# A Newton-iteration and spectral-convolution kernel: earlier loads and another cadence for the inverse transforms, and filler matmuls at the end

## The chip, the cores and the metric

The kernel runs on one core of a Trainium2 chip. The metric is the device time of one execution in microseconds (us), taken as the median of several runs; lower is better. All data is 32-bit floating point.

## What is computed

The input `x` holds 32 images of 32 channels of 128 x 128 numbers. Two layers follow each other, each a residual step on a group-normalised input:

```
def _L0_conv_ref(A):                       # a matrix square root for each 128x128 channel
    normA = jnp.sqrt(jnp.sum(A2 * A2, axis=(1, 2)))
    Y = A2 / normA[:, None, None]; Z = I
    for _ in range(5):
        T = 0.5 * (3.0 * I - jnp.matmul(Z, Y))
        Y = jnp.matmul(Y, T)
        Z = jnp.matmul(T, Z)
    return Y * jnp.sqrt(normA)[:, None, None]

def _L1_conv_ref(x, weights1, weights2):   # a spectral convolution, 32 modes each way
    x_dht = jnp.fft.fftn(x.astype(jnp.complex64), axes=(2, 3)).real
    top = jnp.einsum('bixy,ioxy->boxy', x_dht[:, :, :M1, :M2], weights1)
    bot = jnp.einsum('bixy,ioxy->boxy', x_dht[:, :, -M1:, :M2], weights2)
    # top and bot are put into an otherwise zero spectrum
    y = jnp.fft.ifftn(out_dht.astype(jnp.complex64), axes=(2, 3)).real
    return y

x = x + _L0_conv_ref(_gn(x))
x = x + _L1_conv_ref(_gn(x), L1_conv_weights1, L1_conv_weights2)
```

## The kernel before, in words

**Layer 0.** The unit of work is a *quad*: four channels of one image, so 256 quads in all. `newton` (L426) carries a quad through a chain of small matrix products on TensorE (PE), whose results VectorE (DVE) and ScalarE (ACT) bring back from PSUM; GpSimd (POOL) adds the identity (`r<-mb,eye`, `r<-b,eye`). It ends with the product `ps<-y,t` and the DVE add `xt<-ps,xt`. `settle` (L458) writes the finished quad to the DRAM scratch `mid` (issued by SP) and folds it on POOL (`fold<-xt`).

**Layer 1.** `forward`, `summed` and `spectrum` make an image's spectrum. The images are cut into groups of 20, 7, 3 and 2 (`GROUPS`, L43). When a group's spectra are complete, `wide_products` (20), `small_products` (7 and 3) or `last_products` (2) multiply them by the weights, mode by mode, and write the products to the DRAM scratch `od`. Then `inverse` (L887) takes the images of the group one by one: `load_products` (SP, `ob<-od` or `or<-od`), `place` (ACT, puts small groups' products in order, `ob<-or`), two banks of matmuls `ps<-tab,ob` copied by ACT to `gt`, and then for each half `e` of the channels eight matmuls `ps<-gt,tab`, ACT copies to `d`, DVE adds `yt<-ps,yt`, and `unfold` (POOL `yt<-yt,d`, 8 channels at a time, two instructions). `store` issues the finished 8 channels to `out`. `yt` are the image's own rows, read back from `mid` by `load_input(b, e)` (L832), two transfers of 512 KB for each half; they come from a pool of six buffers, in turn.

**What sets the order.** Nothing is scheduled at run time: every engine gets its instructions in the order in which the Python program issues them (`InOrder`, L68), and each engine, SP's queue too, holds at an instruction whose semaphores are not ready. The program is a loop of *rounds* (L1042 on). In each round every lane (up to nine, at most five quads under way in the last images) gives one step of its quad, and in between one step each of the queues `preps`, `specs`, `posts`, `prods` (the products) and `backs` (the inverses) is taken. The last images start a quad every 5 rounds (`NEAR`). A step of `inverse` ends at each `yield`. Before, these lines set the pace:

```
            if i == 0 and rounds % 3 or tail:
                step(prods)
            if i == 0 and (rounds % 3 == 0 or holding) or tail and not (posts or specs):
                step(backs)
```

so `backs` has every third round and, by `holding`, the round after the first quarter of each half; `prods` has the other two rounds. An image of a group takes six steps: one in which it only sees that its loads were issued, one for `ps<-tab,ob`, and two for each half. Counting through the loop this makes 12 rounds an image. The second half's rows are loaded at the end of the first half (`if not e: load_input(b, 1)`), two rounds ahead of the DVE adds that use them. `tail` is true once no quad is left or under way: then every queue is stepped for each lane. Stores are issued by SP, in the tail by ACT.

**Buffers that matter at the end.** `page` is a pool of three tiles shared by `om` (products on their way to `od`), `d` and `or`. PSUM is a ring of eight banks (`bank`). While the last quads run, `weights` (L782) also sends 28 weight tiles of 256 KB through SP's queue into Newton buffers that have come free.

Of the kernel before, what the change touches and what calls it, by code (L numbers as in the profile page):

```python
# [88 lines left out]
def conv_preact_kernel(  # L89
# [77 lines left out]

    def bank():
        return ps8.tile([P, 4, P], F32, tag="ps", name="ps")

    def root(v, n, tag):

# [154 lines left out]
    def products(lhsT, rhs):  # L327
        ps = bank()
        for j in range(4):
            nc.tensor.matmul(ps[:, j, :], lhsT[:, j], rhs[:, j], start=True, stop=True)  # L330
        return ps
# [94 lines left out]
    def newton(g, sn, xt, m, mb, far, more):  # L426


        q = yield from quartic(m, mb, far, more, False)
        my = four("my", more)  # L430
        y = my[:, :, 0, :]
        nc.scalar.mul(y, products(q, m), 1 / (MS * QF))
        yield from rest
        m = my[:, :, 1, :]
        nc.scalar.mul(m, products(q, y), MS / QF)
        yield from rest
        mb = taken(transposed(m), "mb", more)
        yield from rest
        q = yield from quartic(m, mb, far, more, True)
        both = [bank().rearrange("p (j k) x -> p j k x", k=2) for _ in range(2)]  # L440
        for j in range(4):
            nc.tensor.matmul(both[j // 2][:, j % 2], q[:, j], my[:, j], start=True, stop=True)
        w, y = four("t", more), four("y4", more)
        for h in range(2):
            nc.scalar.mul(w[:, 2 * h : 2 * h + 2, :], both[h][:, :, 1, :], 1 / (MS * QF))
        for j in range(4):
            c = 4 * g + j
            nc.scalar.mul(y[:, j, :], both[j // 2][:, j % 2, 0, :], sn[:, c : c + 1])
        yield from rest
        t = plus(products(w, q), -0.5 * EYE / (1.5 * QF), eye, "t", more)  # L450
        yield from rest
        nc.vector.tensor_tensor(xt, products(t, y), xt, ALU.add)
        yield

    folds = {}
# [88 lines left out]
    def spectrum(b, u):  # L544


        uv = u.rearrange("p q c a (t e l) -> p a e t (q c) l", e=2, l=4)
        ps = [bank() for _ in range(2)]
        for a in range(2):
            for i in range(2):  # L550
                for e in range(2):
                    rows = slice(64 * i, 64 * i + 64)
                    nc.tensor.matmul(
                        ps[i][64 * e : 64 * e + 64, 0:2, :],
                        tab[rows, T_FH.start + a * K : T_FH.start + (a + 1) * K],
                        uv[rows, a, e],
                        start=(a == 0),
                        stop=(a == 1),
                    )
        z = sp.tile([P, 4, P], F32, tag="sp", name="z", bufs=2)  # L560
        for i in range(2):
            nc.scalar.copy(
                z.rearrange("p t (l i c) -> p t l i c", i=2, c=G)[:, :, :, i, :],
                ps[i].rearrange("p a x -> p (a x)")[:, 0:256].rearrange(
                    "p (t c l) -> p t l c", c=G, l=4
                ),
            )
        yield
        v, r = scales.pop(b)
        ps = transposed(z)  # L570
        spec = sp.tile([P, 4, P], F32, tag="sp", name=f"spec{b}", bufs=2)
        spec = spec.rearrange("p a x -> p (a x)").rearrange("p (k q t) -> p k q t", q=4, t=8)
        nc.scalar.activation(
            spec.rearrange("p k q t -> p t (k q)"),
            ps.rearrange("p t (e k) -> p (t e) k", e=2),
            AF.Identity,
            scale=r,
        )
        yield
        nc.vector.scalar_tensor_tensor(  # L580
            spec[0:C, 0, 0, 0:1], v[0:C, 1:2], r[0:C], spec[0:C, 0, 0, 0:1], ALU.mult, ALU.add
        )
        yield
        i, j = where[b]
        if i == len(xs):

            for e, t in enumerate(diags):
                for l4 in range(4):
                    rows = slice(32 * l4, 32 * l4 + 32)
                    copy = nc.scalar.copy if l4 % 2 else nc.vector.tensor_copy  # L590
                    copy(
                        t.rearrange("p (m b l f) -> p m b l f", b=2, l=4, f=4)[rows, :, j, l4, :],
                        spec[rows, 8 * e : 8 * e + 8].rearrange("p k q (h f) -> p (k q h) f", f=4),
                    )
            yield
            return
        kept(
            nc.sync.dma_start(
                out=xs[i][:, :, j, :].rearrange("k p m -> p k m"),
                in_=spec.rearrange("p (k e) q t -> p k (e q t)", e=KK // xs[i].shape[0]),  # L600
            )
        )
        yield
# [136 lines left out]
    def last_products(i):  # L740


        for e in range(2):
            load_input(B - GROUPS[i], e)
        for kk in range(KK):
            if kk % 4 == 0:
                yield
                om = page(f"om{i}_{kk}").rearrange("p (f s o) -> p s f o", f=4, s=8)
            if kk % 2 == 0:
                pm = bank()  # L750
            for h in range(2):
                if kk < 2:
                    wt = plain[kk][:, 512 * h : 512 * h + 512].rearrange("p (q x) -> p q x", q=4)
                else:
                    wt = late_wts[2 * kk - 4 + h]
                for q in range(4):
                    m = 8 * (kk % 8) + 2 * q + h
                    nc.tensor.matmul(
                        pm[32 * q : 32 * q + 32, 2 * (kk % 2) + h, :],
                        diags[kk // 8][:, 32 * m : 32 * m + 32],  # L760
                        wt[:, q, :],
                        start=True,
                        stop=True,
                    )
            if kk % 2:
                half = kk % 4 // 2
                copy = nc.vector.tensor_copy if half else nc.scalar.copy
                copy(
                    om[:, 4 * half : 4 * half + 4], pm.rearrange("p s (f o) -> p s f o", f=4)
                )  # L770
            if kk % 4 == 3:
                for f in range(4):
                    queue = nc.scalar if f % 2 else nc.sync
                    kept(
                        queue.dma_start(
                            out=od[i][f, kk - 3 : kk + 1].rearrange("k r x -> r k x"),
                            in_=om[f::4, :, f, :].rearrange("p (k h) o -> p k (h o)", h=2),
                        )
                    )
        yield  # L780

    def weights():  # L782
# [49 lines left out]
    def load_input(b, e):  # L832

        if b >= B or (b, e) in yts:
            return
        yts[b, e] = []
        for i in range(2):
            o = 16 * e + 8 * i
            turn = len(yts) + i
            if len(settled) == B * C // 4 and not folds and turn % 3 == 2:  # L840
                y = sets.tile([P, 8, P], F32, tag="fold", name=f"yt{b}_{o}", bufs=3)
            else:
                y = inv.tile([P, 8, P], F32, tag="yt", name=f"yt{b}_{o}", bufs=6)
            kept(nc.sync.dma_start(out=y, in_=mid[b][:, o : o + 8, :]))
            yts[b, e].append(y)
# [3 lines left out]
    def store():  # L849
        while stores:  # L850
            b, o, y = stores.pop(0)
            kept((nc.scalar if tail else nc.sync).dma_start(out=out[b, :, o : o + 8, :], in_=y))
# [34 lines left out]
    def inverse(b):  # L887


        more = where[b][1] < GROUPS[where[b][0]] - 1  # L890
        load_products(b)
        load_input(b, 0)
        yield
        if b not in placed:
            place(b)
            if not tail:
                yield
# [12 lines left out]
        for e in range(2):  # L910
            gts.append(inv.tile([P, 4, P], F32, tag="gt", name=f"gt{b}_{e}", bufs=3))
            nc.scalar.copy(gts[e], pg[e])
        unfold()
        yield
        for e in range(2):
# [16 lines left out]
            for i in range(2):  # L932
# [11 lines left out]
                if not i:  # L944
                    holding.append(b)
                    yield
                    holding.pop()
            if not e:
                load_input(b, 1)
            elif more:  # L950
                load_input(b + 1, 0)
                place(b + 1)
            yield
        if not more:
            unfold()
# [86 lines left out]
    while todo or any(lanes) or posts or specs or prods or backs:  # L1042
# [3 lines left out]
        for i in range(LANES):  # L1046
# [26 lines left out]
                step(specs)  # L1073
            if i == 3 or tail:
                step(posts)
            if i == 0 and rounds % 3 or tail:
                step(prods)
            if i == 0 and (rounds % 3 == 0 or holding) or tail and not (posts or specs):
                step(backs)
        rounds += 1  # L1080

# [68 lines left out]
```

## Time and profile before

Every instruction is recorded through one helper, so all have line L83 (`keep_in_program_order`) and are told apart by the tiles that they write and read.

| | |
|---|---|
| median of 3 runs | 3040.89 us (3040.22 to 3058.99) |
| the profiled execution's own time | 3037.9 us |
| its span on the core | 3035.8 us |
| PE busy, weight loads apart | 2878.3 us, 95% of the span |
| DVE, POOL, ACT busy | 2263.7, 1987.6, 1644.0 us |
| POOL `yt<-yt,d` | 242 instructions, 304.3 us, 1280 ns each |
| DVE `yt<-ps,yt` | 256 instructions, 682 ns each (median) |
| mean granted TensorE clock | 0.983 |

In the timeline a row gives the start, the duration, the engine, the operation with its tiles and shapes, how many equal instructions it merges, and in brackets the engine's idle time before it and what ended that. SPq and ACTq rows are the issuing of transfers. The windows view gives, for each stretch, its length and then each engine's busy time and instruction count, the granted clock, the DMA engines' mean share and GB/s.

### The profile page before, as it was taken

How to read it: one execution, taken by the hardware profiler on the slowest of the kernel's cores; microseconds unless marked ns; L12 is line 12 of the kernel's file. 1: busy time of each engine (PE TensorE's matmuls, PEld its weight loads, DVE VectorE, ACT ScalarE, POOL GpSimd, SP SyncE). 2: the span in 40 equal slices, each digit the busy share in tenths (PEclk: the TensorE clock that was granted, in tenths of full speed). 3: DMA queues.
4: the chain of work that ended last, by engine and by line, in shares of the span. 5: the costliest groups of instructions: out<-in, count | busy, mean ns of one | idle time of the engine just before them, and what ended most of it. 6: DMA issues, size and time to landing. Idle time of an engine off the chain costs nothing. (4 is left out here: it accounts for less than half of the span.)

```text
span 3035.8 us, 73213 instructions
## 1 busy us (share of the span) xinstructions
PE 2878.3 (95%) x27076; PEld 2675.2 (88%) x27076; DVE 2263.7 (75%) x4261; ACT 1644.0 (54%) x4187; POOL 1987.6 (65%) x2306
## 2 busy tenths in 40 slices
PE   6999999999999999999999999999999999898973
PEld 6899999999999999999999889889888889797863
DVE  6778787878787888778876656877778767776654
ACT  3566565665656665565644445555555555564442
POOL 4577677777777776767765435678777774675542
PEclk9999999999999999999999999999999999999986
DMA  5576676777675768575733567667667677575585
GB/s 173 163 231 206 213 215 214 215 214 222 201 232 189 240 190 247 182 240 185 246 109 105 169 205 233 234 215 254 235 205 258 230 249 241 178 233 179 183 265 187
DMA packets 476658, 636.39 MB, mean 210 GB/s; under 512 B 97040, under 2 KB 257296, under 8 KB 476304
## 3 DMA queue, kind: packets, MB, share of 16 engines
q1 hardware_dynamic: 362400, 422.21, 43.3%
q10 hardware_dynamic: 113904, 209.50, 22.3%
q8 instruction: 217, 3.56, 0.5%
q14 instruction: 137, 1.12, 0.1%
HBM read 402.42 MB, written 229.11 MB: 208 GB/s over the span
## 5 line engine op out<-in xcount | busy, mean ns | idle before, releaser
L83 PE MATMUL ps<-my,q 128*128 128x128 f32 (+1 forms) x4096 | 736.4, 329 | 12.7 <-DVE v L83 9.8
L83 PEld LDWEIGHTS ps<-my,q 128*128 128x128 f32 x4096 | 625.8, 191 | 71.5 <-DVE v L83 11.4
L83 POOL TENSOR_TENSOR w<-w,r 128x512 f32<-128x512 f32 x288 | 366.7, 1275 | 379.2 <-DMA w<-turn 308.7
L83 PE MATMUL ps<-w,v 128*128 128x128 f32 x4096 | 552.5, 278 | 25.1 <-DVE w L83 12.4
L83 ACT ACTIVATE b<-b,a_off,a_sc 128x128 f32<-128x128 f32 x1024 | 469.8, 492 | 173.1 <-issue 47.5
L83 POOL TENSOR_TENSOR fold<-xt 128x256 f32<-128x256 f32 x512 | 363.3, 731 | 285.0 <-DVE xt L83 256.2
L83 PEld LDWEIGHTS ps<-w,v 128*128 128x128 f32 x4096 | 503.2, 193 | 40.0 <-DVE w L83 11.8
L83 ACT ACTIVATE my<-ps 128x512 f32<-128x512 f32 x512 | 306.1, 604 | 351.1 <-PE ps L83 333.7
L83 DVE SCALAR_TENSOR_TENSOR q<-ps,eye 128x512 f32<-128x512 f32 x512 | 350.4, 685 | 180.6 <-PE ps L83 175.8
L83 POOL TENSOR_TENSOR yt<-yt,d 128x512 f32<-128x512 f32 x242 | 304.3, 1280 | 273.1 <-ACT d L83 240.7
L83 ACT ACTIVATE t<-ps 128x256 f32<-128x256 f32 x512 | 191.2, 382 | 356.6 <-PE ps L83 345.7
L83 POOL TENSOR_TENSOR r<-mb,eye 128x512 f32<-128x512 f32 x256 | 326.3, 1275 | 79.1 <-ACT mb L83 79.1
L83 POOL TENSOR_SCALAR x<-xt,a_nm,a_sc 128x128 f32<-128x128 f32 x736 | 321.6, 450 | 21.3 <-DVE a_n L83 18.7
L83 POOL TENSOR_TENSOR r<-b,eye 128x512 f32<-128x512 f32 x256 | 326.5, 1275 | 2.7 <-ACT b L83 2.7
L83 ACT ACTIVATE y<-ps,a_t_s 128x128 f32<-128x128 f32 x1024 | 291.2, 375 | 0.0
L83 PE MATMUL ps<-x,b 128*128 128x128 f32 x2048 | 274.9, 278 | 7.5 <-POOL x L83 5.7
L83 PE MATMUL ps<-x,q 128*128 128x128 f32 x2048 | 274.4, 277 | 4.0 <-DVE q L83 2.2
L83 PE MATMUL ps<-y,t 128*128 128x128 f32 x2048 | 273.8, 277 | 2.3 <-DVE t L83 2.3
L83 PE MATMUL ps<-my,mb 128*128 128x128 f32 x2048 | 273.6, 277 | 0.4 <-DVE q L83 0.4
L83 PE MATMUL ps<-q,t 128*128 128x128 f32 x2048 | 274.1, 277 | 0.0
L83 DVE STREAM_TRANSPOSE turn<-v 128x512 f32<-128x512 f32 x288 | 264.9, 920 | 9.9
L83 PEld LDWEIGHTS ps<-x,b 128*128 128x128 f32 x2048 | 251.3, 193 | 11.0 <-POOL x L83 6.0
(121 smaller groups left out, 4481.1 us busy)
## 6 DMA issues: line engine op xcount, KB each, us to landing
turn<-turn SPq DMA_DIRECT2D x288, 256.0 KB
b<-in_x ACTq DMA_DIRECT2D x256, 256.0 KB
xt<-in_xt ACTq DMA_DIRECT2D x256, 256.0 KB
xs<-in_xs ACTq DMA_DIRECT2D x256, 256.0 KB
mid<-xt SPq DMA_DIRECT2D x256, 256.0 KB
yt<-mid SPq DMA_DIRECT2D x128, 512.0 KB
out<-yt SPq DMA_DIRECT2D x113, 512.0 KB
w<-turn SPq DMA_DIRECT2D x144, 256.0 KB
```

Source lines behind the costliest of these rows:

```text
L83: return self.tc.keep_in_program_order(issue(*args, **kw))
```

## The change

The inverses get fixed rounds of ten (0, 3 and 7) instead of every third. A step that only waited for loads is dropped for all images but the first of a group, so an image takes five steps, which is 10 rounds. The second half's rows are loaded in the step of the image's first matmuls, ahead of which the stores that are ready are issued; stores are also issued after a `holding` round. In the tail the two last images' products are loaded together and placed before the first one's output. `warm(n)` puts n matmuls of 128 x 512 whose results nobody reads into TensorE's queue: 2 after the last quad's last product, 2 ahead of the last group's products, 9 after them.

```
+    def warm(n):
+        ps = bank()
+        for _ in range(n):
+            nc.tensor.matmul(ps, ident, tab[:, 0:512], start=True, stop=True)
...
         nc.vector.tensor_tensor(xt, products(t, y), xt, ALU.add)
+        if not todo and lanes.count(None) == LANES - 1:
+            warm(2)
         yield
...
+            if tail:
+                warm(2)
             yield
             return
         kept(
...
+        warm(9)
         yield
 
     def weights():
...
         more = where[b][1] < GROUPS[where[b][0]] - 1
-        load_products(b)
-        load_input(b, 0)
-        yield
         if b not in placed:
+            load_products(b)
+            if tail and more:
+                load_products(b + 1)
+            load_input(b, 0)
+            yield
             place(b)
...
             nc.scalar.copy(gts[e], pg[e])
+        if tail and more:
+            place(b + 1)
+        store()
+        load_input(b, 1)
         unfold()
         yield
...
                     yield
                     holding.pop()
-            if not e:
-                load_input(b, 1)
-            elif more:
+                    store()
+            if e and more:
                 load_input(b + 1, 0)
-                place(b + 1)
+                if b + 1 not in placed:
+                    place(b + 1)
             yield
...
-            if i == 0 and rounds % 3 or tail:
+            turn = rounds % 10 in (0, 3, 7)
+            if i == 0 and not turn or tail:
                 step(prods)
-            if i == 0 and (rounds % 3 == 0 or holding) or tail and not (posts or specs):
+            if i == 0 and (turn or holding) or tail and not (posts or specs):
                 step(backs)
```

## The prediction

> **What bounds the kernel now.** I read the page first, then windows cut at each image's first inverse matmul, then the timeline at TensorE's three largest late gaps.
>
> ```profile
> span 3035.8 us, 73213 instructions
> PE 2878.3 (95%) x27076; PEld 2675.2 (88%) x27076; DVE 2263.7 (75%) x4261; ACT 1644.0 (54%) x4187; POOL 1987.6 (65%) x2306
> ...
> PE   6999999999999999999999999999999999898973
> PEclk9999999999999999999999999999999999999986
> ```
>
> TensorE is full until the last two slices, so in the body only its idle time can be won; after about 2939 us it is idle for long stretches and its clock falls. In the inverses' stretch I cut windows from one image's `ps<-tab,ob` to the next's:
>
> ```profile
> 1934.50:1962.20 27.70, 27.70 (x251) 25.27 (x250) 20.24 (x40) 15.38 (x42) 21.82 (x26) 1.00 0.68 233
> 2086.50:2116.10 29.60, 29.60 (x259) 26.83 (x258) 24.07 (x52) 16.01 (x43) 22.89 (x27) 1.00 0.77 265
> 2180.00:2217.10 37.10, 31.53 (x259) 28.51 (x258) 28.11 (x44) 17.36 (x48) 24.19 (x30) 0.91 0.58 188
> 2247.60:2277.80 30.20, 30.20 (x267) 27.60 (x266) 19.98 (x35) 16.30 (x43) 24.68 (x29) 1.00 0.75 248
> 2400.10:2430.80 30.70, 30.41 (x265) 27.37 (x264) 27.19 (x53) 16.37 (x44) 24.78 (x29) 1.00 0.66 222
> ```
>
> These are images 2, 7, 10, 12 and 17. Length less PE busy is idle time: 0 to 0.3 us in four, 5.6 us in image 10, where the next images' statistics fall on POOL's `yt<-yt,d`. Over images 0 to 25, less 19 (its window holds products), the idle time adds up to 34 us. The largest gap comes after image 26's first half:
>
> ```profile
> 2787.94 2.36 SPq L83 DMA_DIRECT2D out<-yt  x3
> ...
> 2791.59 2.17 SPq L83 DMA_DIRECT2D yt<-mid  x2
> ...
> 2799.80 1.29 DVE L83 TENSOR_TENSOR yt<-ps,yt 128x512 f32<-128x512 f32 x2 [11.55 <-DMA yt<-mid]
> ...
> 2801.74 3.69 PE L83 MATMUL ps<-my,q 128*128 128x256 f32 x8 [9.83 <-DVE v L83]
> ```
>
> The second half's load left SP late, behind the small group's `diag<-xs` issues and three stores; DVE waited at its head, a Newton step's `v` stood behind it, and TensorE starved. The same happens to image 28 at the last quad:
>
> ```profile
> 2938.51 2.35 SPq L83 DMA_DIRECT2D out<-yt  x3
> 2941.16 5.83 SPq L83 DMA_DIRECT2D yt<-mid  x2
> ...
> 2950.03 1.29 DVE L83 TENSOR_TENSOR yt<-ps,yt 128x512 f32<-128x512 f32 x2 [11.72 <-DMA yt<-mid]
> ...
> 2954.32 1.40 POOL L83 TENSOR_TENSOR fold<-xt 128x256 f32<-128x256 f32 x2
> 2955.77 1.97 PE L83 MATMUL ps<-fold,tab 128*32 128x504 f32 x12 [16.25 <-POOL fold L83]
> ```
>
> After that all is one chain to the end: spectrum, products, `od` and back, two inverses.
>
> ```profile
> 2980.85 9.06 SPq L83 DMA_DIRECT2D od<-om  x6
> 2987.91 0.59 ACT L83 COPY om<-ps 128x512 f32<-128x512 f32 x1 [9.86 <-DMA od<-om]
> ...
> 2997.30 3.07 SPq L83 DMA_DIRECT2D or<-od  x4
> ...
> 3003.01 1.05 ACT L83 COPY ob<-or 128x512 f32<-128x512 f32 x1 [6.58 <-DMA or<-od]
> ...
> 3016.85 2.08 PE L83 MATMUL ps<-tab,ob 64*128 64x128 f32 x16 [6.45 <-DVE ob L83]
> ```
>
> The third `om` waits for a page whose write to `od` stood in SP's queue behind image 30's loads; the last image's matmuls wait until `ob` is placed at the very end of the one before.
>
> **What the Trainium skill says.** "TensorE: Matmul & The Clock Gate", section "The HAM clock gate": an idle window of about 3.4 us halves TensorE's clock until it has been busy about as long. The trace agrees: after the 16 us gap the twelve fold matmuls take 1.97 us, where a like group took 1.09 at 2911.70. "SBUF — State Buffer", section "SBUF: two separate sides": VectorE with two SBUF inputs and GpSimd lock one port pair for a whole instruction. It agrees: DVE's 128 x 1 `b_inv` takes 4.34 us at 1917.29, beside POOL's `yt`, and 0.16 us at 2883.24. "DMA: Bandwidth & Descriptors", section "Issuing engines are not separate DMA queues": so a store moved to ACT frees SP, not bandwidth.
>
> **The change part by part**, against the profiled execution's 3037.9 us (span 3035.8; the rest lies around it).
>
> *Image 26's stall.* Its first-half end moves from round 964 to 951, ahead of the group's products (from 962), and its second load is issued six rounds, some 15 us, before use. Gone: 9.83 us of gap, and the eight `my,q` after it at half clock, 3.69 against 1.89 us: **-11.6**.
>
> *Cadence.* The total number of rounds stays 1032, and the work is the same; it is denser. 10 rounds are two quads, so every image now meets the quads in one phase. That phase (first half's matmuls at a round divisible by 5, POOL's `yt` 1, 3, 4 and 7 rounds on) is exactly that of images 2, 7, 12 and 17 before: near zero idle. The three statistics steps, in rounds 663, 743 and 903, now all come right behind a `yt`: about 5 us each where they cost 2.0, 5.6 and 4.5. So of 34 us perhaps 20 to 34 stay; ends -14 and, if density costs 1 us an image, +13. I take **-3**.
>
> *Products.* Seven rounds of ten let three products follow each other; a weight buffer reloaded two rounds before use must land in about 6 us, of which SP's four issues take 2.5 us and the matmuls 1.2. Five of the 32 wide steps have this; ends 0 and 2 us each, less the 2.34 us of the first, which gets one round more. I take **+3**.
>
> *The last quad.* Image 28's second rows are issued near 2932 instead of 2941 and used near 2939 to 2940. `t`, `ps<-y,t` and `xt` follow by 2945. Late next is POOL: it stands with four `yt` (2.5 us each) and one fold ahead of the last fold, from about 2936, so the last fold ends near 2948.3 and TensorE's fold matmuls start there instead of 2955.8: **-7.5**. `warm(2)` and image 29's `ps<-tab,ob` lie in that wait.
>
> *Clock.* A 128 x 512 matmul costs some 0.9 us (half of it a 128 x 256: 1.89 us for 4), twice that at half clock. If the clock holds, fold, spectrum, transposes and first products save 0.9 + 0.9 + 0.5 + 0.9; if not, the second `warm(2)` takes 3.7 us in a 2.2 us gap and costs 1.5. I take **-1.6**.
>
> *The `om` wait*, 2970.3 to 2987.9. Stores now go out earlier, so three of image 30's four loads are issued before the products; the fourth needs image 28's last buffer, stored by ACT behind two `od`. ACT 1.5 + 0.4, store 4.0, SP 0.4 + 1.2, landing 3: 10.5 instead of 17.6: **-7.1**. From there to the `ob` copy, 15.1 before: without image 29's loads between the `od` writes some 13.7: **-1.4**.
>
> *`warm(9)`*: 8.5 us warm, 11 when it starts cold, 16.6 cold throughout. From the third `om` copy to the placed `ob` are 14.8 us (13.7 + 1.1), which hide it; cold throughout it would cost 2.
>
> *The two last images.* From the `ob` copy (3003.0) to DVE's end (3031.3) were 28.3 us. With both placed, the second's matmuls hide behind DVE: 4.1 us to the first add (two copies, 1.2 + 1.2 of matmuls warm), 16 adds of 0.62, four pairs of DVE `yt<-yt,d` of about 2.3: 23.1. **-5.2**.
>
> Sum: -11.6 - 3 + 3 - 7.5 - 1.6 - 7.1 - 1.4 - 5.2 = -34.4, so 3003.5 for the profiled execution; the median stood 3 us above it: **3007 us**.
>
> **Rivals.** *Only the stalls go* (chance 0.22): the `od` writes still queue and the clock stays halved. Then -11.6 - 7.5 + 3: 3025 us. For it: the store that the fourth load needs still sits on the chain. *The body's idle goes as well* (0.13): -14 instead of -3, products free: about 2993 us; the four images speak for it, the statistics steps against. *Early loads are late anyway* (0.04): buffers come from stores of two halves before, and SP holds at POOL's `yt` ahead of them; then little but the end is won: 3026 us. Against: the six buffers give each load its buffer two to three rounds earlier. *The one phase is a bad one* (0.06), the slower side: POOL's `yt` in front of `r`, and `w` behind it, at every image. If each of 27 images lost what image 10 lost, 5.6 us against 1.3 on average, that is +116, near 3122 us; above 2.5 us more an image it outweighs the whole gain. Against it stand the same four images.
>
> **How the numbers follow.** Likeliest 3007 (0.55), its own range 2998 to 3018. One per cent is 30.4 us, about what a measurement of this kernel can tell from no change; the bound is 3010.5. Faster: 0.55 x 0.72 + 0.13 = 0.53; slower 0.06; within 0.41. The range, 2993 to 3026, leaves out the bad phase and the outer ends.
>
> **What would show it.** After: no DVE wait on `yt<-mid` above 5 us; TensorE's fold matmuls 7 us nearer the last `ps<-y,t`; the span between the second and third `om` near 10 us; `ps<-tab,ob` of the last image without a gap; PE idle in the statistics steps alone. It is wrong if `ps<-diag,plain` shows DMA gaps of several us, or if DVE `w` waits for POOL `r` by more than the 56.1 us that the waits view gives now.

## The result, and the profile after

| | before | after |
|---|---|---|
| median | 3045.48 us (3040.22 to 3058.99, 4 runs) | 3012.28 us (3008.09 to 3015.97, 4 runs) |
| ratio of after to before | | 0.9884, 95% interval 0.9846 to 0.9922 |
| the same ratio, timed again later (7 and 4 runs) | | 0.9887, 95% interval 0.9870 to 0.9903 |
| the profiled execution's own time, its span | 3037.9, 3035.8 us | 3008.1, 3006.3 us |

After is 1.1 to 1.2% faster, and its median lies inside the range given. Both intervals reach across 0.99, so that the gain exceeds the one per cent named in the prediction is likely but not shown. The kernels were timed in five sets of runs, each beside before. The median of before alone moved between 3038 and 3049 us from one set to the next, so kernels of different sets are compared here by their ratios to before.

The page of after, span, busy times and TensorE's two rows of slices:

```profile
span 3006.3 us, 73268 instructions
PE 2891.6 (96%) x27102; PEld 2680.5 (89%) x27102; DVE 2260.4 (75%) x4259; ACT 1639.7 (55%) x4187; POOL 1990.1 (66%) x2308
...
PE   6999999999999999999999999999999999999995
PEclk9999999999999999999999999999999999999997
```

The dips in the last slices of TensorE's row are gone but for the last, which rose from 3 to 5: the end is shorter, not full. PE's busy time rose by 13 us; the filler matmuls alone are 16.8 (3.60, 3.48 and 9.69 in the timeline).

Image 26's second half, where DVE had stood for 11.55 us at the add (timeline of after):

```profile
2759.73 1.61 PE L83 MATMUL ps<-gt,tab 32*128 32x260 f32 x16
...
2762.64 1.27 DVE L83 TENSOR_TENSOR yt<-ps,yt 128x512 f32<-128x512 f32 x2
```

No bracket, so no idle time ahead of the add: the rows were there. The last quad and the tail, also of after:

```profile
2933.63 2.53 DVE L83 TENSOR_TENSOR yt<-ps,yt 128x512 f32<-128x512 f32 x4 [6.38 <-DMA yt<-mid]
2936.90 2.05 PE L83 MATMUL ps<-y,t 128*128 128x128 f32 x8 [8.09 <-DVE t L83]
2938.74 3.60 PE L83 MATMUL ps<-tab,ident 128*128 128x512 f32 x4
2940.31 1.40 POOL L83 TENSOR_TENSOR fold<-xt 128x256 f32<-128x256 f32 x2
2942.27 1.16 PE L83 MATMUL ps<-tab,ob 64*128 64x128 f32 x16
2943.36 1.09 PE L83 MATMUL ps<-fold,tab 128*32 128x504 f32 x12
2964.22 0.58 ACT L83 COPY om<-ps 128x512 f32<-128x512 f32 x1 [3.64 <-DMA od<-om]
2976.43 1.05 ACT L83 COPY ob<-or 128x512 f32<-128x512 f32 x1 [5.10 <-DMA or<-od]
2988.23 3.80 PE L83 MATMUL ps<-gt,tab 32*128 32x260 f32 x32 [3.98 <-ACT gt L83]
```

DVE's wait at image 28 is smaller but not gone (6.38 against 11.72 us); the fold matmuls run at full clock (1.09 against 1.97 us), but behind the first `warm(2)` (`ps<-tab,ident`, 3.60 us at half clock) and image 29's `ps<-tab,ob`; and the last image's `ps<-gt,tab` still has a gap of 3.98 us.

**Where the time went.** The trace can be cut at the ends of the quads, `xt<-ps,xt` on DVE. The 153rd (quad 152, counted from 0) ends ahead of everything that the change touches; quads 152 to 168 cover the first group's products, 168 to 224 its twenty inverses, 224 to 248 the second group. For every kernel of this study, lengths in us. In the column of quads 168 to 224 the brackets hold TensorE's summed gaps (the length less its busy time) and its time at half clock:

| kernel | 152-168 | 168-224 | 224-248 | 248-255 | 255 to the end | ratio to before, 95% interval |
|---|---|---|---|---|---|---|
| before | 204.3 | 740.4 (23.4, 13.7) | 333.7 | 80.7 | 83.9 | 1 |
| after | 208.2 | 750.3 (25.6, 23.9) | 311.1 | 79.8 | 66.6 | 0.9884 (0.9846-0.9922) |
| after, again (e12) | 208.2 | 740.2 (21.0, 10.2) | 311.8 | 79.4 | 66.5 | 0.9887 (0.9870-0.9903) |
| e1 load and stores only | 202.3 | 748.9 (29.3, 23.9) | 328.0 | 79.3 | 77.9 | 0.9965 (0.9952-0.9978) |
| e2 cadence only | 208.7 | 726.7 (13.7, 0) | 311.5 | 85.3 | 77.9 | 0.9897 (0.9876-0.9917) |
| e3 tail only | 204.3 | 747.4 (28.2, 17.1) | 333.8 | 80.6 | 83.2 | 1.0007 (0.9995-1.0019) |
| e4 after, no fillers | 208.3 | 742.4 (21.6, 13.7) | 312.8 | 79.4 | 70.4 | 0.9894 (0.9872-0.9917) |
| e5 after, late load in first group | 208.0 | 745.7 (24.9, 13.7) | 312.8 | 80.2 | 67.7 | 0.9875 (0.9859-0.9891) |
| e6 cadence and tail | 209.0 | 729.6 (15.3, 3.4) | 311.1 | 83.7 | 72.8 | 0.9857 (0.9839-0.9875) |
| e7 cadence only, other phase | 211.0 | 738.5 (21.1, 13.7) | 314.9 | 85.3 | 71.3 | 0.9905 (0.9891-0.9920) |
| e8 every third round, five steps | 202.5 | 740.0 (18.8, 23.9) | 317.9 | 85.8 | 73.5 | 0.9904 (0.9887-0.9920) |
| e9 no early load or stores in first group | 208.7 | 730.7 (14.7, 6.8) | 313.1 | 80.0 | 67.2 | 0.9851 (0.9831-0.9870) |
| e10 one store less in first group | 207.4 | 732.2 (15.0, 10.2) | 311.7 | 79.4 | 66.2 | 0.9849 (0.9831-0.9866) |
| e11 e9, products in two of three rounds | 203.0 | 735.1 (17.8, 6.8) | 311.1 | 79.4 | 67.3 | 0.9857 (0.9840-0.9874) |

Each row is one profiled execution. How far they can be trusted shows in stretches that the edits leave alone: quads 168 to 224 differ by 10.1 us between the two profiles of after, and up to quad 152, where all kernels do the same work, the profiles take 1590.3 to 1601.8 us. Shorter columns repeat within about 2 us.

From before to after the span lost 29.5 us: 2.5 ahead of quad 152, where both do the same work, +3.9, +9.9, -22.6, -0.9, and -17.3 after the last quad. The gain sits in the second group and in the tail; the first group, where the new cadence was to help a little, gave 0 to 10 us back.

### The profile page after: what moved, and what is told of

Same layout as the page of the kernel before. It is cut to its first block, busy times and chain, and to the rows that moved or that the text cites. A ratio compares the mean times of both kernels' runs of the same rounds, so it can differ in the third digit from the quotient of the medians.

```text
span 3006.3 us, 73268 instructions
## 1 busy us (share of the span) xinstructions
PE 2891.6 (96%) x27102; PEld 2680.5 (89%) x27102; DVE 2260.4 (75%) x4259; ACT 1639.7 (55%) x4187; POOL 1990.1 (66%) x2308
## 3 DMA queue, kind: packets, MB, share of 16 engines
q10 hardware_dynamic: 113616, 208.45, 22.2%
## 5 line engine op out<-in xcount | busy, mean ns | idle before, releaser
L83 PEld LDWEIGHTS ps<-my,q 128*128 128x128 f32 x4096 | 626.4, 192 | 67.1 <-ACT my L83 10.2
L83 PE MATMUL ps<-w,v 128*128 128x128 f32 x4096 | 552.1, 278 | 16.8 <-DVE w L83 8.2
L83 PEld LDWEIGHTS ps<-y,t 128*128 128x128 f32 x2048 | 253.3, 193 | 14.1 <-issue 8.6
```

The costliest lines, as they stand in the source:

```text
L83: return self.tc.keep_in_program_order(issue(*args, **kw))
```

## The experiments

The first theory: the early load brings the body's gain, the tail part and the earlier stores bring the tail's, and the first group pays for early loads at which SP holds. The main rival: the cadence is what counts, for good or ill. The change falls into three parts; four kernels take them one by one, or take the fillers away.

**e1, the load part alone**: before, with the second rows loaded in the step of the first matmuls and both new `store()` calls.

```
             nc.scalar.copy(gts[e], pg[e])
+        store()
+        load_input(b, 1)
         unfold()
...
                     holding.pop()
-            if not e:
-                load_input(b, 1)
-            elif more:
+                    store()
+            if e and more:
```

> The kernel before with the early second-half load and its earlier stores alone; every third round, six steps an image and the old tail are kept. Theory (the gain of the body and of the om wait comes from the load): image 26's DVE wait on yt<-mid goes, about -11 us; image 28's shrinks, -3; the om wait shrinks by about 7; SP holding at loads whose buffer is not stored gives back up to 5: 14 to 22 us faster than before. Rival A (the load needs the denser rounds, because the stores free buffers too late): image 26's or another image's wait on yt<-mid stays above 5 us and the gain is under 8 us. Rival B (the hold of SP that stops ACT's loads through shared completion semaphores is the price): ACT shows my waits of 7 to 9 us here too, and the gain is under 14.

Measured: ratio 0.9965, about 10.6 us faster. Image 26's wait is gone (224 to 248: -5.7), the wait of the third `om` is 12.5 us instead of 17.6. The gain is smaller than the 14 to 22 us that the theory wanted, and neither rival explains it: DVE has no wait for `yt<-mid` left, and no wait of ACT's `my` is longer than 4.7 us, where rival B had 7 to 9.

**e2, the cadence alone**: three of ten rounds and five steps an image; second rows loaded as before, old tail.

```
+            turn = rounds % 10 in (0, 3, 7)
-            if i == 0 and rounds % 3 or tail:
+            if i == 0 and not turn or tail:
...
-        load_products(b)
-        load_input(b, 0)
-        yield
         if b not in placed:
+            load_products(b)
+            load_input(b, 0)
+            yield
             place(b)
```

> The kernel before with rounds 0, 3 and 7 of ten and five steps an image alone; second half's rows are still loaded at the end of the first half, old tail. Theory (density costs about 5 us in the first group, by reloads of weights two rounds before use and by one image's work packed into fewer rounds, and saves nothing by itself but image 26's place in the order): -6 to +6 us against before. Rival (the denser rounds themselves are what the first group loses): +8 to +20 us, with the loss between quads 160 and 216. If the cadence were the source of the gain: below -8.

Measured: ratio 0.9897, about 31 us faster, as much as the whole change. The theory had given the cadence -6 to +6 us and is wrong. By column, from before to e2, the lengths change by +4.4, -13.7, -22.2, +4.6 and -6.0 us. The windows view of the two stretches, e2 first and then after (length, then each engine's busy time with its instructions, clock, DMA share, GB/s):

```profile
1810.60:2537.30 726.70, 713.02 (x7272) 648.79 (x7272) 546.80 (x1012) 383.33 (x985) 514.63 (x610) 1.00 0.75 240
2537.30:2848.80 311.50, 305.82 (x3563) 279.75 (x3562) 224.41 (x406) 175.00 (x420) 207.13 (x250) 0.99 0.67 211
```

```profile
1798.50:2548.80 750.30, 724.66 (x7273) 659.09 (x7273) 545.58 (x1012) 381.42 (x985) 514.69 (x610) 0.98 0.71 233
2548.80:2859.90 311.10, 304.76 (x3563) 278.65 (x3562) 224.66 (x405) 174.57 (x420) 207.14 (x250) 1.00 0.65 211
```

The second lines agree: in the second group the early load adds nothing to the cadence. The first lines don't: the same matmuls take 23.6 us less without the load part, 12 of it in gaps (length less PE busy: 13.7 against 25.6) and 12 in matmuls at half clock (PE busy 713.0 against 724.7). Against the second profile of after (740.2 us) it is 13.5 us less.

**e3, the tail part alone**: before, with `warm` and its three calls, and both last images' products loaded and placed together (these lines stand in the diff above).

> The kernel before with the tail's part alone: both last images' products loaded and placed together and the 2 + 2 + 9 filler matmuls. Theory: -5 from the last image (its ps<-tab,ob stand in no gap), -2 from a full clock at fold, spectrum and first products, the om wait of some 17 us stays as it was because it hangs on image 30's loads and stores: 5 to 10 us faster than before. Rival (the om wait was the tail's gain too): 12 to 18 us faster, second to third om near 10 us. Rival (fillers cost what they save): 0 to 4 us faster.

Measured: ratio 1.0007, nothing; of the three forecasts only the rival of the costly fillers (0 to 4 us faster) is met by the interval. Its timeline shows why:

```profile
3000.06 10.85 PE L83 MATMUL ps<-tab,ident 128*128 128x512 f32 x18 [11.00 <-ACT om L83]
3010.84 1.15 PE L83 MATMUL ps<-gt,tab 32*128 32x260 f32 x16
3012.06 1.29 DVE L83 TENSOR_TENSOR yt<-ps,yt 128x512 f32<-128x512 f32 x2 [10.13 <-PE ps L83]
3018.52 1.05 ACT L83 COPY ob<-or 128x512 f32<-128x512 f32 x1 [4.76 <-DVE yt L83]
```

`warm(9)` starts at half clock and lasts 10.85 us, and behind it in PE's queue stand image 29's own `ps<-gt,tab`, for which DVE waits 10.13 us. The `ob` copy then comes 19.1 us after the third `om` (2999.43), instead of 15.1. From the `ob` copy to DVE's end it then takes 25.0 us, as in after, instead of 28.3. So the placing gave 3.3 us, and the wait behind `warm(9)` took 4.0. (The placing without fillers was not run by itself.) In after the cadence has image 29's matmuls done ahead of `warm(9)`, and the filler is covered.

**e4, after without fillers**: `warm` returns at once.

> The kernel after without any filler matmul. Theory: the clock halves in the gap after the last ps<-y,t and for the whole tail; fold, spectrum and first products lose about 2 us, the last two images' ps<-tab,ob and ps<-gt,tab another 1 to 2, and the second warm(2), which after ran at half clock on the path, gives 1 us back: 1 to 4 us slower than after. Rival (the tail waits for ACT, DVE and transfers, and TensorE's clock hardly matters): within 1 us of after. Rival (fillers stand in the way): 1 to 3 us faster than after.

Measured: ratio 0.9894 against 0.9884 and 0.9887 for after. In the profiles the tail takes 70.4 us without the fillers and 66.6 or 66.5 with them; from the fold matmuls to the second `om` it is 14.9 against 12.0 us. Ahead of that the fillers cost something: the fold matmuls start 2.1 us after the last `xt` without them, 3.7 and 2.9 us in the two profiles of after, where `warm(2)` stands in front. In all the profiles speak for 4 us, and the times can't tell it from nothing. The fold matmuls of e4, held by POOL's `fold` alone and at half clock:

```profile
2940.95 1.97 PE L83 MATMUL ps<-fold,tab 128*32 128x504 f32 x12 [0.80 <-POOL fold L83]
```

The theory in its first form had fallen: the cadence carries the body, and the load part costs something in the first group. Next: what exactly of the load part costs, whether the phase matters, and which half of the cadence does it.

**e5, after, second rows of the first group loaded late again.**

```
         store()
-        load_input(b, 1)
+        if GROUPS[where[b][0]] <= NB:
+            load_input(b, 1)
...
-            if e and more:
+            if not e:
+                load_input(b, 1)
+            elif more:
```

> The kernel after, but in the first group of 20 images the second half's rows are loaded at the end of the first half again (stores and everything else as in after). Theory (in the first group the early load makes SP hold at a load whose buffer is still being stored, ACT's loads then hold behind it, and TensorE starves): the stretch from quad 168 to quad 224 falls from 742 to 750 us to about 727, as with the cadence alone; 10 to 20 us faster than after, near 2996. Rival (the earlier stores, not the load, make SP hold): within 4 us of after. Rival (the tail needs what after loses in the body, so that the end comes at the same time): body 15 us shorter, time within 4 us of after.

Measured: 745.7 us in the first group, no shorter. So the load is not what costs; the rival, the stores, is left.

**e6, cadence and tail without the load part.**

> The kernel before with the cadence and the tail's part, without the early load and its earlier stores. Theory (the load part costs 10 to 20 in the first group, but gives the tail some 8 us by the second to third om wait): 3000 to 3010, near the cadence alone less 1 to 4. Rival (the tail's gain of after is the tail part's own): 8 to 12 us faster than the cadence alone. Rival (the tail part is worth nothing, as it was alone on the kernel before): within 2 us of the cadence alone.

Measured: ratio 0.9857, better than after by 0.3% (some 9 us), as the theory's two prices together had it: the first group takes 729.6 us. The tail is 72.8 us against 77.9 of the cadence alone, so on top of the cadence the tail part is worth about 5 us, unlike alone. By the ratios e6 is even 12 us faster than the cadence alone, where the theory had 1 to 4 and the rival 8 to 12; the last two columns of the profiles show 6.7 of them. After's last two columns are another 10 us shorter than e6's, so the tail's gain is not the tail part's alone.

**e7, the cadence alone in another phase**: `turn = rounds % 10 in (2, 5, 9)`.

> The cadence alone, with the inverses in rounds 2, 5 and 9 of ten instead of 0, 3 and 7: the same density, another phase against the quads. Theory of the prediction (the phase is what makes the images' idle time near zero; others lose up to 5.6 us an image): 15 to 60 us slower than the cadence alone, DVE's w waits longer for POOL's r. Rival (only density and the earlier place of image 26 count): within 5 us of the cadence alone.

Measured: ratio 0.9905 against 0.9897, intervals that overlap; the 15 to 60 us of the theory are out. The first group's profile is 11.8 us longer, with three gaps of 3.5 to 4.9 us, but that is hardly more than two profiles of one kernel differ by. DVE's `w` waits 37.1 us for POOL's `r` over the run, against 24.3 in e2.

**e8, five steps in every third round**: `turn = rounds % 3 == 0`, nine rounds an image.

> Five steps an image, but in every third round as before: nine rounds an image, denser than after, and with a phase that moves against the quads. Theory (phase and density of ten rounds give the gain together): faster than before by 10 to 25, since image 26 leaves the products' loads, but slower than the cadence alone by 5 to 20, with gaps in the images at bad phases. Rival (the dropped step alone counts): within 4 us of the cadence alone or faster.

Measured: ratio 0.9904, 29 us faster than before and within 2 us of the cadence alone, as the rival had it. Five steps an image bring this in ten rounds of either phase and in nine rounds with a moving phase. Here `w` waits 60.6 us for `r`, more than the 56.1 of before, in a kernel 1% faster: that wait alone doesn't set the time. In the profiles of e7 and e8 the gain lies behind the first group, which takes 738.5 and 740.0 us, hardly less than in before; e8's profile is the slowest of its five runs.

**e9 and e10** look for the store. e9 leaves out all of the load part in the first group. e10 keeps it, but for one call:

```
                     holding.pop()
-                    store()
+                    if GROUPS[where[b][0]] <= NB:
+                        store()
```

> The kernel after, but in the first group of 20 images neither the early load nor the earlier stores; both stay in the later groups and the tail. Theory as it now stands (the earlier stores, which the early load needs, make SP hold at POOL's yt; ACT's loads of xs hold behind SP's, my comes late and TensorE starves): quad 168 to quad 224 in 727 to 731 us instead of 742 to 750, later stretches as in after (312, 80, 67): some 15 us faster than after in the profile, ratio to before 0.983 to 0.985. Rival (what is won in the first group is lost again later, in the last quad or the tail): ratio 0.987 to 0.989, as after.

> The kernel after without the one store() behind the holding round, in the first group only; the early load and the store() in front of it stay there. If that store is what makes SP hold: quad 168 to 224 near 730 us. If the store() in the step of the first matmuls and the load behind it do: 742 to 750, ratio to before as after's, 0.987 to 0.989, and PE's gaps at ps<-my,q behind an ACT my that waited for a DMA stay.

Measured: 730.7 and 732.2 us in the first group, ratios 0.9851 and 0.9849, medians 2993.89 and 2992.74 us (before beside them 3038.12). Taking away the one `store()` after the holding round brings back as much as taking away the whole load part, and nothing of it is lost again later. The load itself is harmless. (An early load without any of the earlier stores wasn't tried: its buffers come free by them.) After and e10 were timed in different sets, on different chips, but the chip alone doesn't explain it: e4 and e2 shared a chip, e5 and e6 another, and there too the kernel with the store takes longer in this stretch, 742.4 against 726.7 and 745.7 against 729.6 us.

How a store that only waits for POOL starves TensorE, at image 8 of after:

```profile
2080.50 0.33 SPq L83 DMA_DIRECT2D out<-yt  x1
2080.88 1.25 SPq L83 DMA_DIRECT2D yt<-mid  x2
2082.18 1.21 SPq L83 DMA_DIRECT2D ob<-od  x2
2086.88 5.58 ACTq L83 DMA_DIRECT2D xs<-in_xs  x3
2092.50 0.60 ACT L83 ACTIVATE my<-ps 128x512 f32<-128x512 f32 x1 [7.98 <-DMA ob<-od]
2093.15 2.08 PE L83 MATMUL ps<-my,q 128*128 128x128 f32 x8 [3.47 <-ACT my L83]
```

and at the same image of e10:

```profile
2075.61 1.45 SPq L83 DMA_DIRECT2D yt<-mid  x2
2077.16 1.09 SPq L83 DMA_DIRECT2D ob<-od  x2
2083.68 4.23 ACTq L83 DMA_DIRECT2D xs<-in_xs  x3
2087.95 0.60 ACT L83 ACTIVATE my<-ps 128x512 f32<-128x512 f32 x1 [5.41 <-PE ps L83]
2088.60 1.16 PE L83 MATMUL ps<-my,q 128*128 128x128 f32 x8 [0.99 <-ACT my L83]
```

In after SP holds at the store until POOL's `yt` ends, at 2080.50, and the next image's loads `yt<-mid` and `ob<-od` leave only then; in e10 they leave 5.3 us earlier by the two traces, 3.2 us when their offset of 2.1 us is taken off (the last `my` ahead of them starts at 2078.30 and 2076.23). They land later too, and ACT's `xs` loads, which have nothing to do with them, wait for that: the releaser named for `my` is the transfer `ob<-od`. The landings of the trace fit to a few hundredths of a us:

```
after:  yt<-mid landed 2086.86, ob<-od landed 2091.34 and 2092.10; ACT issued its three xs<-in_xs at 2086.88, 2091.36, 2092.12
e10:    ob<-od landed 2085.47, out<-yt landed 2087.52;             ACT issued its last two xs<-in_xs at 2085.49, 2087.55
```

In this program the transfers of SP and ACT take eight completion semaphores in turn, and each waits for the last user of its own: in the trace of after the three `xs` loads wait for and take the very semaphores that one `yt<-mid` and the two `ob<-od` had taken. So a late transfer of SP's holds ACT, with the `my` of a quad behind it. In e10 ACT is held too, until `out<-yt` lands, but its `my` starts 2.5 us sooner, the offset of the traces taken off.

This is one of a few such places. Over the first group's twenty images TensorE's gaps of 0.9 us and more at `ps<-my,q` behind an ACT `my` are 3.09, 3.47 and 1.92 us in after, 1.08, 3.51 and 1.15 in e12, and one of 0.99 in e10. They often cost the clock as well: it is at half for 6.8 us after this one. In all TensorE's gaps are 10.6 and 6.0 us longer than in e10, of which these are 7.5 and 4.8; the others were not followed back to their causes.

**e11, e9 with the first group's products in two of three rounds** (`rounds % 3 if len(settled) < 200 else not turn`).

> As the kernel without both in the first group, and the first group's products again in two of three rounds, so that no weight tile is reloaded only two rounds before its use. Theory of the prediction (those reloads cost +3): quad 152 to 168 in 203 to 205 us instead of 208, the rest unchanged: 2 to 6 us faster than the one without it. Rival (the 48 rounds of the products instead of 46 only move that time to the next stretch): within 2 us.

Measured: 203.0 instead of 208.7 us for the products, as the theory had it, but 735.1 instead of 730.7 in the next stretch, and ratios 0.9857 against 0.9851. The rival was right in the time, which is the same within 2 us; that it moves to the next stretch is what one profile shows.

**e12, after again.**

> The kernel after, unchanged, timed again in more rounds, because its ratio's interval (0.9846 to 0.9922) still overlaps that of the version without the one store (0.9831 to 0.9866). If that store is worth what the profiles say (12 to 18 us between quads 168 and 224): ratio 0.988 to 0.991, and that stretch 742 us or more again. If the first profile of after was a bad one: ratio 0.984 to 0.986, the stretch near 732.

Measured: ratio 0.9887, as expected if the store costs, and 740.2 us in the stretch, just under the 742 expected then and 8 us above e10. The interval (0.9870 to 0.9903) no longer meets that of e10 (0.9831 to 0.9866), so e10 beats after by about 0.4%, 12 us. Its ratio is the lowest of the study; those of e9, e6 and e11 lie within its interval.

## Why the prediction was nearly right, point by point

The forecast of 3007 us stood 5 us below the measured median; the sum of -34.4 us stands against -29.5 in the span. That is closer than its parts were, and so in part luck: first group, second group and last quad were each off by 7 to 13 us in the profile, in both directions.

- **Image 26's stall, -11.6: right, and too small.** The gap of 9.83 us and the half clock are gone. But quads 224 to 248 gained 22.6 us: two gaps of 2.15 and 2.24 us at image 20 and several of 1.0 to 1.7 us went as well (gaps 25.3 to 6.3 in all, half clock 10.2 to 0). The reason given, the load issued six rounds ahead, was only half of it. The cadence alone does all this (311.5 us), by the other half of that sentence: the first half's end moves ahead of the group's products. The load alone removes the stall too, and gains 5.7 us.
- **Cadence, -3: wrong, and the reading of four windows behind it.** "Exactly that of images 2, 7, 12 and 17 before: near zero idle" did not hold: over images 0 to 18 TensorE idles 23.7 us in after and 23.2 in before, and single images, all in that phase now, still idle up to 4.2 us. The rival built on that phase also has a slip: it would have eaten the whole gain at 1.3 us more an image (34.4 over 27 images), not at 2.5. Without the load part the cadence brings the first group from 740.4 to 726.7 us; e7 and e8 put two other rhythms within 0.1% of it in time, so the phase is not shown to matter. In after the `store()` behind the holding round takes 8 to 18 us of it back. That store is the failed step: the text counted "stores now go out earlier" as a gain in the tail and never asked which loads stand behind it in SP's queue during twenty images, nor that ACT's loads depend on SP's landings. Of the rivals, "SP holds at POOL's `yt`" named the place, but as a cause for late loads of the image, not of `xs`.
- **Products, +3: right in size** (+3.9, 208.2 against 204.3, with a gap of 3.43 us at `ps<-diag,plain`, the sign that the prediction named for being wrong, but only one), and e11 shows that undoing it buys nothing.
- **The last quad, -7.5: wrong.** From quad 248 to 255 after gained 0.9 us, and from the end of the last `xt` to the fold matmuls it takes 3.7 us as before (3.9). The first of these two has a cause that the sum put at nothing: with five steps an image and no load part (e2, e6, e7, e8) quads 248 to 255 take 83.7 to 85.8 us, in all other kernels 79.3 to 80.7. So the load part does win 4 to 6 us here, and the cadence costs them. The load left at 2926.05, early as forecast, but landed only at 2933.51, 7.5 us later, beside the transfers of the weight tiles (from 2924 to 2940 the DMA engines' mean share is 1.0); DVE's wait fell to 6.38 us, not below 5. POOL, called late next, was not: its fold ran at 2940.31. In its place the fold matmuls waited for `warm(2)`, which was to lie in POOL's wait: without fillers (e4) they start after 2.1 us.
- **Clock, -1.6: right in sign.** Fold matmuls to second `om`: 14.5 before, 12.0 after, 14.9 without fillers. The second `warm(2)` ran cold (3.48 us) and held the products back by about 1 us, the case priced at 1.5.
- **`om` wait, -7.1: 17.6 became 8.8**, -8.8. The load part brings 5 of it (12.5 in e1), the cadence 3 (14.8 in e2), the tail part nothing (17.2 in e3).
- **Third `om` to `ob` copy, -1.4:** 15.1 became 12.2.
- **`warm(9)` hidden: right in after** (9.69 us, before the placed `ob`), where the cadence has image 29's matmuls ahead of it; in e3 it stands on the path.
- **The two last images, -5.2:** 28.3 became 25.0, -3.3. The second's `ps<-tab,ob` stand in no gap, but its `gt` copies are behind ACT's `d` copies: the 3.98 us gap above.

So the tail, from the clock on, was forecast at -15.3 and measured at -17.3; body, products and last quad were forecast at -19.1 and measured at -9.7; the other -2.5 lie ahead of the change. Rival "only the stalls go" (3025) was refuted by the tail; "the body's idle goes as well" (2993) is about what e9 and e10 reach, 2994 and 2993 us.

## What to carry to other kernels

An instruction put earlier into a queue that holds in order is paid by what stands behind it: ask, for a store that waits for another engine, which loads come next in its queue, in every stage and not only in the one that it is meant for. Take a change of several parts apart before believing which one pays: here one part alone gave as much as the whole, one part gave nothing by itself because its fillers stood in front of real work, and one `store()` of a third cost, by the times, more than the rest of that part gave.

## What the runs showed of the hardware

A queue can be held by a transfer of another queue to other memory. The Trainium skill, "DMA: Bandwidth & Descriptors", section "Anatomy of one DMA — SWDGE (gpsimd) path", says that the transfer engines don't wait on semaphores and that any such wait happens on the issuing sequencer. The trace agrees, for SP's and ACT's queues: ACT issued three loads in 5.58 us and did nothing else in that time, each let go within 0.03 us of a landing.

The same 512 KB of `yt<-mid` landed 6.0 us after its issue at 2080.88 and 10.9 us after it at 2084.73: its size alone doesn't tell how late a load may leave. And gaps of 2 to 3.5 us in a stream that is otherwise full were enough to halve the clock for 3.4 to 6.8 us, but not each time: one gap of 2.1 us at `ps<-x,q` (2003.3 in after) stands in the first group of all kernels with rounds 0, 3 and 7 of ten, and was followed by half clock in after, e12, e4, e5, e9 and e10, by none in e2, e6 and e11. The profiles with over 18 us of gaps in the first group had 10 to 24 us at half clock there, those with fewer 0 to 10.
